# V's bias in the first group: from one-row matmuls on TensorE to the VectorE step that empties PSUM

## The chip, the core and the metric

The kernel runs on one core of a Trainium2 chip. Five engines work on their own instruction queues, each in the order in which the program lists them: TensorE (PE in the profile; its weight loads are PEld), VectorE (DVE), ScalarE (ACT), GpSimd (POOL) and SyncE (SP), which only starts transfers between the chip's memory and SBUF here. The metric is device time in microseconds (us) of one execution; less is better.

## The reference

One graph attention layer over 128 samples of 128 nodes with 768 features, 12 heads of 64, all in float32:

```python
h = jnp.maximum(_layernorm(x, axis=-1), 0.0)
q, k, v = split_heads(h @ Wq + bq), split_heads(h @ Wk + bk), split_heads(h @ Wv + bv)
scores = einsum('bhqd,bhkd->bhqk', q, k) / sqrt(HD) + beta * adj
scores = where(adj > 0, scores, -9e15)
x = x + einsum('bhqk,bhkd->bhqd', softmax(scores), v)
```

The change concerns `h @ Wv + bv` for the first 4 samples, and a preparation of the three weight matrices that is done once.

## The kernel before

**Groups and slices.** The samples are taken in 32 groups of 4 (512 rows). Each group goes through three slices: `qk0` (the first half of the heads' Q and K), `v` (all of V) and `qk1` (the other half of Q and K). Scores, exponentials and the weighted sums of the heads are slipped between the products of later slices.

**Two ways of multiplying.** From the second group on, each slice is a Strassen-like scheme: 15 products (`PRODUCTS`, `product_z`, L543) of sums of activation blocks with sums of weight blocks. The first group is multiplied plainly (`plain_slice`, L832), because the sums of the weights do not exist yet. While TensorE does that, the other engines make them (`prepare`, L271), for `qk0`, `v` and `qk1` in turn: 27 steps a slice, of which 12 are sums on VectorE (`sums`, L297, through L305 and L307) and 15 are finishes (`finish`, L309, and `rest`, L283). Each finish fills the remaining seventh parts of one product's weight tile: two small VectorE sums (L284 and L285, 128x128 each) and two GpSimd sums (L289, L290). The products named B01, B21 and B22 use raw weight blocks; for them `rest` first copies three 128x128 blocks (L287 takes two, L288 one), on GpSimd. Of each slice's 15 tiles, 11 in all three together stay in SBUF (`RESIDENT`); the others are written to memory on SyncE's queue (L293) and read back in each later group. In `v` the tiles are finished in the order T9, T12, T11, TX, T2, B01, B21, B22, T6, T1, T0, T7, T4, T13, T10, where the numbers `n` in `PRODUCTS` are 0, 1, 14, 4, 2, 6, 9, 13, 5, 12, 10, 7, 8, 11, 3.

**The order.** From the first group's `v` slice on, the order of each engine's instructions is that of the program, which is written out by hand in slots. A plain slice has 18 slots: 6 result blocks (two rows of samples by three column blocks) of 3 partial products each. After each third of a block, `behind_product` and the `todo` lists put the other engines' work of that slot into their queues. In the `v` slice: slot 0 to 3 one preparation step, after that two a slot; in slots 5 to 12 one of eight loads each of the raw weights of `qk1` (`raw_qk1_piece`, L246 to L249, in turn from Wq and Wk, 288 KB each); rows of a later group are loaded in slots 0, 1, 2 and 6 and summed on ScalarE (`row_stats`, L421 to L423) in slots 5, 7, 9 and 12; the layer norm's moments of the second group in slots 9 and 12 (`moments_1`, `moments_2`, L375 to L398). All these loads and the writes of prepared tiles share SyncE's queue, in that order. The `qk0` slice, ahead of it, is not ordered by hand.

**One block of V.** TensorE sums 24 matmul passes into a pair of PSUM banks (L855; there are four such pairs in rotation, `take` and `give`). After the first third, two matmuls with one row of ones as weights and the bias as data add the bias to the two halves (L860; float32 takes each in two passes, so four instructions are listed). At the end ScalarE copies the block to SBUF (L871) and the pair is free again. Blocks of Q and K get their bias in the ScalarE step that copies them out (L877). In later groups V's bias is added by VectorE out of PSUM (L573).

**What follows.** The `qk1` slice of the first group multiplies by the raw weights that the eight loads brought: within each third of a block, first all of Wq's part, then all of Wk's. Its preparation starts in slot 16 of the `v` slice with a sum over both. Then the second group begins with L559, whose activation sums VectorE makes at L476.

Of the kernel before, what the change touches and what calls it, by code (L numbers as in the profile page):

```python
# [10 lines left out]
F32 = mybir.dt.float32  # L11
# [3 lines left out]
ALU = mybir.AluOpType  # L15
AX = mybir.AxisListType

P = 128
HEADS = 12
GRP = 4  # L20
# [108 lines left out]
def direct(ctx, tc, x, adj, wq, bq, wk, bk, wv, bv, beta, out, bad):  # L129
# [10 lines left out]
    nc = tc.nc  # L140
    B, N, D = x.shape
    HD = D // HEADS
# [12 lines left out]
    const = ctx.enter_context(tc.tile_pool(name="const", bufs=1))  # L155
# [40 lines left out]
    for g in range(2):  # L196
        t = xg[0, g]
# [6 lines left out]
    mean8 = flat(spot + P, spot + 2 * P).rearrange("p (a i) -> p a i", i=SQ)  # L204
    nhalf = const.tile([P, 1], F32, name="nhalf")
    nc.gpsimd.memset(nhalf, -0.5)
    ones = const.tile([P, P], F32, name="ones")
    nc.gpsimd.memset(ones, 1.0)
    tiny = const.tile([P, 1], F32, name="tiny")
    nc.gpsimd.memset(tiny, TINY)  # L210
# [3 lines left out]
    NS = 2 * NG + 1  # L214
    seen = const.tile([P, NS], F32, name="seen")

    over = const.tile([P, NS + 24], F32, name="over")
# [50 lines left out]
    def quarters(t):  # L268
        return t[:, 0:6].rearrange("p (c z) n -> p c z n", c=2)[:, :, 0:2]

    def prepare(sl):  # L271

        def home(name):
            n = [i for i, p in enumerate(PRODUCTS) if p[1] == name][0]
            if (sl, n) in resident:
                return resident[sl, n]
            made_in[0] += sl != "qk1"
            if sl != "qk1" and made_in[0] % 8 in (2, 5, 7):
                t = work.tile([P, 2, W], F32, tag="e", name=f"prep_{sl}_{n}", bufs=3)
                return t.rearrange("p i w -> p (i w)")[:, 0:7 * P].rearrange("p (z n) -> p z n", n=P)  # L280
            return work.tile([P, 7, P], F32, tag="T", name=f"prep_{sl}_{n}", bufs=RING)

        def rest(n, t, b11, b12, b22, b=None):  # L283
            nc.vector.tensor_tensor(t[:, 6], b12, b11, ALU.subtract)  # L284
            nc.vector.tensor_tensor(t[:, 2], b22, b12, ALU.add)  # L285
            if b is not None:
                nc.gpsimd.tensor_copy(t[:, 0:2], b[:, 0])  # L287
                nc.gpsimd.tensor_copy(t[:, 3], b[:, 1, 0])  # L288
            nc.gpsimd.tensor_tensor(t[:, 4], t[:, 1], t[:, 6], ALU.add)  # L289
            nc.gpsimd.tensor_tensor(t[:, 5], t[:, 0], t[:, 4], ALU.subtract)  # L290
            if (sl, n) not in resident:
                k = kept[sl, n] = dram.tile([P, 7, P], F32, name=f"kept_{sl}_{n}")
                nc.sync.dma_start(k, t)  # L293

        made = {}

        def sums(name):  # L297
            for out, a, b, sign in SUMS_B:
                if out == name:
                    if out not in made:  # L300
                        made[out] = home(out)
                    at = [quarters(made[q]) if q in made else wt[sl, q] for q in (a.strip("-"), b)]
                    op = ALU.add if sign > 0 else ALU.subtract
                    if a[0] == "-":
                        nc.vector.scalar_tensor_tensor(quarters(made[out]), at[0], -1.0, at[1], op0=ALU.mult, op1=op)  # L305
                    else:
                        nc.vector.tensor_tensor(quarters(made[out]), at[0], at[1], op)  # L307

        def finish(name):  # L309
            n = [i for i, p in enumerate(PRODUCTS) if p[1] == name][0]  # L310
            if name in made:
                t = made[name]
                rest(n, t, t[:, 3], t[:, 4], t[:, 1])
            else:
                t, b = home(name), wt[sl, name]
                rest(n, t, b[:, 1, 0], b[:, 1, 1], b[:, 0, 1], b)

        steps = []
        for first, then_finish in PREPARED:
            for name in first:  # L320
                steps.append(lambda name=name: sums(name))
            if sl == "qk1" and first[0] == "T0":
                steps += [load_T, load_T]
            for name in then_finish:
                steps.append(lambda name=name: finish(name))
        return steps
# [28 lines left out]
    bv_b = const.tile([P, D], F32, name="bv_b")  # L355
# [164 lines left out]
    def turn():  # L520

        while between and next(between[0], None) is None:
            between.popleft()
# [4 lines left out]
    def home_qk(G, sl, r, j, zones=False):  # L528
        t = home_of[G, sl, r, j] = homes.popleft()
        return t if zones else t[:, 0:4].rearrange("p (i g) n -> p i (g n)", i=2)  # L530
# [275 lines left out]
    def trail():  # L806
        while trailing:
            trailing.popleft()()

    def behind_product(at, todo):  # L810
        pending = [masking.popleft() for _ in range(len(masking))]
        for f in pending:
            f()
        for f in todo.get(at, ()):
            f()
        while weighing:
            weighing.popleft()()
        overdue()
# [13 lines left out]
    def plain_slice(G, sl, todo, rows=(0, 1)):  # L832

        n = 0
        row0 = None
        for r in rows:
            for j in range(3):
                row0 = last if (r, j) == (1, 0) and sl == "qk0" else row0
                bank = take()
                p = bank[:, :, 0:H2]  # L840

                parts = (slice(0, N), slice(N, H2)) if sl == "qk0" and r == j == 0 else (slice(0, H2),)
                for at, k in [(at, k) for at in parts for k in range(3)]:
                    a, b = A[G, f"A{r}{k}"], wt[sl, f"B{k}{j}"]
                    for i in range(2):
                        for c in range(2):
                            lhs, rhs = b[:, c, i], a[:, c, at]
                            if sl == "v":
                                lhs, rhs = a[:, c, i * N:(i + 1) * N], b[:, c].rearrange("p i n -> p (i n)")
                            for q in range(0, P, HD) if sl == "qk1" else (slice(0, P),):  # L850
                                q = slice(q, q + HD) if sl == "qk1" else q
                                with ExitStack() as behind:
                                    if sl == "qk0" and r == 1:
                                        behind.enter_context(tc.issue_after(row0.ins))
                                    last = nc.tensor.matmul(p[q, i, at], lhs[:, q], rhs, start=(k == 0 and c == 0),  # L855
                                                            stop=(c == 1), skip_group_check=True)
                            turn()
                    if sl == "v" and k == 0:
                        for i in range(2):
                            nc.tensor.matmul(p[:, i], ones[0:1], bv_b[0:1, j * 2 * P:(j + 1) * 2 * P], start=False,  # L860
                                             stop=True, skip_group_check=True)
                    if at is not parts[-1]:
                        if k == 1:
                            with tc.issue_after(last.ins):
                                second()
                        continue
                    if k == 2:
                        if sl == "v":
                            t = vt[G, sl, r, j] = vring[nv[0] % len(vring)]
                            nv[0] += 1  # L870
                            nc.scalar.copy(t.rearrange("p (g h) e -> p g h e", g=2)[:, :, :, 0:HD],  # L871
                                           p.rearrange("p g (h d) -> p g h d", d=HD))
                        else:
                            t = qk[G, sl, r, j] = home_qk(G, sl, r, j)
                            oc = j + 3 * int(sl[2])
                            for i in range(2):
                                nc.scalar.activation(t[:, i, :], p[:, i, :], AF.Identity, bias=bqk[:, i, oc:oc + 1])  # L877
                        give(bank)
                    behind_product(n, todo)
                    trail()  # L880
                    for f in todo.get((n, "post"), ()):
                        f()
                    n += 1
# [163 lines left out]
    for n in range(5, 18):  # L1047
        then(n, after, step, 2)
    plain_slice(0, "qk0", todo)

    ordered = ctx.enter_context(ExitStack())
# [16 lines left out]
    for g, at in enumerate((5, 7, 9, 12)):  # L1068
        then((at, "post"), row_stats, 2, g)
    then((14, "post"), add_raw, 1)  # L1070
    plain_slice(0, "v", todo)

    todo.clear()
# [92 lines left out]
        part()  # L1166

    pf = take()
    nc.tensor.matmul(pf[0:1, 0, 0:NS + 24], ones[:, 0:1], over, start=True, stop=True)
    nc.vector.tensor_reduce(bad, pf[0:1, 0, 0:NS + 24], AX.X, ALU.max)  # L1170
    ordered.close()

# [128 lines left out]
```

## Time and profile before

| | |
|---|---|
| time, median of 3 runs | 2682.6 us (2680.27 to 2682.84) |
| the profiled execution's own time | 2680.71 us |
| its span | 2678.9 us |
| TensorE busy | 2652.9 us (99%) |
| VectorE, ScalarE, GpSimd busy | 2179.0, 1749.4, 2072.5 us |
| mean granted TensorE clock | 0.998 |
| first group: `qk0`, `v`, `qk1` on TensorE | about 10 to 46, 46 to 86, 86 to 123 us |

Times in the profile's rows are counted from the span's start. A row of the timeline gives start, duration, engine, line, operation, output and inputs, and how many instructions were merged; in brackets stands how long the engine stood idle before it and for whom it waited. "PEldq" and "SPq" are the sequencers of TensorE's weight loads and of SyncE. `sbig` is the tile that holds the raw weights, among others; `pair` is a pair of PSUM banks; `kept_v` is the memory copy of a prepared tile.

### The profile page before, as it was taken

To read this page: it belongs to the slowest core of one execution; us is meant where nothing else is said; L and a number is where in the kernel's file an instruction comes from. 1 tells how busy PE (TensorE), PEld (TensorE's weight loads), DVE (VectorE), ACT (ScalarE), POOL (GpSimd) and SP (SyncE) were. 2 spreads that over 40 slices of the span, in tenths; PEclk is the share of its full clock that TensorE was granted. 3 is DMA by queue.
4 is the path that set the end of the run, shared out by engine and by line. 5 is a ranking of instruction groups with operands and counts; after the bars stand their busy time and mean duration, and the time that the engine had idled before them with its cause. 6 is when DMAs were issued, how large, how long until landed. Compare 5 with 4: busy or idle time off the path is not lost.

```text
span 2678.9 us, 121522 instructions
## 1 busy us (share of the span) xinstructions
PE 2652.9 (99%) x52051; PEld 2564.7 (96%) x52051; DVE 2179.0 (81%) x2701; ACT 1749.4 (65%) x4608; POOL 2072.5 (77%) x3043
## 2 busy tenths in 40 slices
PE   9999999999999999999999999999999999999998
PEld 8799999999999999999999999999999999999997
DVE  6877888878888788888788887788887888877885
ACT  2567766676666677666766666776667676667654
POOL 5877778877778777788777787777887777877774
PEclk9999999999999999999999999999999999999999
DMA  9888888989888998889898888988898988888875
GB/s 238 283 261 282 275 270 277 277 265 284 276 271 273 267 279 273 273 277 279 265 281 279 270 272 271 283 274 270 277 277 266 283 277 271 272 274 276 257 240 163
DMA packets 530341, 721.71 MB, mean 269 GB/s; under 512 B 105980, under 2 KB 374024, under 8 KB 529800
## 3 DMA queue, kind: packets, MB, share of 16 engines
q1 hardware_dynamic: 528640, 713.12, 86.7%
q8 instruction: 411, 6.73, 1.0%
q10 hardware_dynamic: 1160, 0.79, 0.2%
q14 instruction: 130, 1.06, 0.1%
HBM read 647.73 MB, written 66.05 MB: 266 GB/s over the span
## 4 chain that ended last, share of the span: by engine, by line
PE 45%; POOL 29%; ACT 13%; issue 5%; DMA 4%; DVE 3%; SPq 0%; POOLq 0%; ACTq 0%; DVEq 0%
PE pair L559 34%; PE pair L695 4%; POOL v L616 4%; PE pair L638 3%; POOL v L615 3%; PE pair L855 3%; POOL A L481 3%; POOL home L614 3%; ACT x L450 3%; ACT e L648 3%; POOL home L601 2%; POOL home L603 2%; ACT home L577 2%; ACT home L579 2%; POOL v L612 2%
## 5 line engine op out<-in xcount | busy, mean ns | idle before, releaser
L583 DVE TENSOR_TENSOR home<-home,pair 128x896 f32<-128x896 f32 x810 | 860.7, 1076 | 273.4 <-PE pair L559 220.7
L559 PE MATMUL pair<-sbig,T_qk 128*64 128x128 f32 x13020 | 833.0, 273 | 1.8 <-DVE sbig L476 0.9
L559 PEld LDWEIGHTS pair<-sbig,T_qk 128*64 128x64 f32 x13020 | 708.2, 137 | 11.6 <-issue 6.4
L559 PE MATMUL pair<-A,T_qk 128*64 128x128 f32 x6944 | 465.6, 273 | 0.4 <-ACT e L707 0.4
L601 POOL TENSOR_TENSOR home<-home 128x256 f32<-128x256 f32 x298 | 246.5, 827 | 268.6 <-DVE home L583 260.1
L678 ACT ACTIVATE e<-e,sm 128x64 f32<-128x64 f32 x1512 | 382.2, 346 | 109.5 <-DVE sm L666 109.5
L559 PE MATMUL pair<-T_v,sbig 128*64 128x128 f32 x6944 | 415.1, 274 | 0.6 <-DMA T_v<-kept_v 0.3
L695 PE MATMUL pair<-v,e 128*64 128x65 f32 x6048 | 401.7, 221 | 6.3 <-DVE e L646 5.9
L577 ACT ACTIVATE home<-pair 128x640 f32<-128x640 f32 x325 | 231.4, 712 | 262.5 <-PE pair L559 201.6
L559 PEld LDWEIGHTS pair<-T_v,sbig 128*64 128x64 f32 x6944 | 380.7, 137 | 12.9 <-issue 10.6
L559 PEld LDWEIGHTS pair<-A,T_qk 128*64 128x64 f32 x6944 | 377.2, 137 | 5.4 <-ACT e L707 4.8
L695 PEld LDWEIGHTS pair<-v,e 128*64 128x64 f32 x6048 | 355.9, 137 | 16.4 <-DVE e L646 12.7
L559 PE MATMUL pair<-sbig,res_qk 128*64 128x128 f32 x4340 | 288.3, 273 | 0.0
L604 POOL TENSOR_TENSOR home<-home 128x256 f32<-128x256 f32 x298 | 238.2, 799 | 23.4
L602 POOL TENSOR_TENSOR home<-home 128x256 f32<-128x256 f32 x298 | 229.8, 771 | 23.4
L559 PEld LDWEIGHTS pair<-sbig,res_qk 128*64 128x64 f32 x4340 | 234.5, 137 | 5.3 <-issue 5.2
L705 ACT ACTIVATE sm<-pair,tiny 128x8 f32<-128x8 f32 x189 | 49.4, 261 | 284.6 <-PE pair L695 284.5
L450 ACT ACTIVATE x<-x,block 128x192 f32<-128x192 f32 x480 | 232.0, 554 | 0.0
L603 POOL TENSOR_TENSOR home<-home 128x128 f32<-128x128 f32 x298 | 213.4, 716 | 23.4
L646 DVE SCALAR_TENSOR_TENSOR e<-pair,biasT 128x1024 f32<-128x1024 f32 x189 | 225.0, 1216 | 2.9 <-PE pair L638 2.8
L648 ACT ACTIVATE e<-e 128x1024 f32<-128x1024 f32 x189 | 193.8, 1066 | 50.2 <-DVE e L646 46.9
L481 POOL TENSOR_TENSOR A<-A 128x256 f32<-128x256 f32 x186 | 168.6, 906 | 56.5 <-DVE A L471 56.5
(201 smaller groups left out, 4598.8 us busy)
## 6 DMA issues: line engine op xcount, KB each, us to landing
T_qk<-kept_qk SPq DMA_DIRECT2D x713, 448.0 KB, 4.8
T_v<-kept_v SPq DMA_DIRECT2D x341, 448.0 KB, 5.6
xo<-in_x_dram SPq DMA_DIRECT2D x189, 256.0 KB, 4.9
out_dram<-xo SPq DMA_DIRECT2D x189, 256.0 KB, 6.0
x<-in_x_dram SPq DMA_DIRECT2D x248, 192.0 KB, 6.2
sbig<-in_x_dram SPq DMA_DIRECT2D x116, 384.0 KB, 3.4
kept_qk<-prep_qk SPq DMA_DIRECT2D x23, 448.0 KB, 3.1
adj<-in_adj_dram SPq DMA_DIRECT2D x128, 64.0 KB, 3.4
```

The source lines that it names most:

```text
L450: nc.scalar.activation(t, t, AF.Relu, bias=shift[G, n], scale=rstd[G, n])
L481: e.tensor_tensor(t[:, 0:2], t[:, 7:8].to_broadcast([P, 2, P]), t[:, 5:7], ALU.subtract)
L559: nc.tensor.matmul(p[q:q + HD, at, :], lhs[:, q:q + HD], rhs, start=(first and at % 4 == 0), stop=True, skip_group_check=True)
L577: nc.scalar.activation(t[:, 0:5], p[:, 0:5], AF.Copy, scale=float(sign))
L583: nc.vector.tensor_tensor(t, t, p[:, 0:7], op)
L601: e.tensor_tensor(t[:, 1:4:2], t[:, 1:4:2], twice(5), ALU.add)
L602: e.tensor_tensor(t[:, 2:5:2], t[:, 2:5:2], twice(1), ALU.add)
L603: e.tensor_tensor(t[:, 4], t[:, 4], t[:, 6], ALU.add)
L604: e.tensor_tensor(t[:, 0:7:6], t[:, 0:7:6], twice(2), ALU.add)
L648: trailing.append(lambda: nc.scalar.activation(e, e, AF.Exp, scale=1.0 / ISCALE))
L678: nc.scalar.activation(o[:, r, b, 0:HD], pa[:, r, b, 0:HD], AF.Copy, scale=t[:, 1, r, b:b + 1])
L695: nc.tensor.matmul(pa[q:q + HD, 2 * g + i, :], k[:, q:q + HD], vt[G, "v", r, h // 4][:, 4 * g + h % 4, :], start=True, stop=True, skip_gro ...
```

## The change

Four edits, all in the first group's part:

- The one-row bias matmuls of the `v` slice are removed; the block is emptied by one VectorE addition of the bias out of PSUM where ScalarE copied it.
- In `rest`, the raw weight copies go from GpSimd to ScalarE, in all three slices.
- In `rest`, for the `v` slice's products with odd `n` (T12, B21, B22, T6, T7, T13 and T10), the second small sum goes from VectorE to GpSimd.
- The tile of ones shrinks from 128 columns to 1; its other use, a sum over partitions at the very end, needs one.

```diff
-    ones = const.tile([P, P], F32, name="ones")
+    ones = const.tile([P, 1], F32, name="ones")
     nc.gpsimd.memset(ones, 1.0)
...
             nc.vector.tensor_tensor(t[:, 6], b12, b11, ALU.subtract)
-            nc.vector.tensor_tensor(t[:, 2], b22, b12, ALU.add)
+            (nc.gpsimd if sl == "v" and n % 2 else nc.vector).tensor_tensor(t[:, 2], b22, b12, ALU.add)
             if b is not None:
-                nc.gpsimd.tensor_copy(t[:, 0:2], b[:, 0])
-                nc.gpsimd.tensor_copy(t[:, 3], b[:, 1, 0])
+                nc.scalar.copy(t[:, 0:2], b[:, 0])
+                nc.scalar.copy(t[:, 3], b[:, 1, 0])
             nc.gpsimd.tensor_tensor(t[:, 4], t[:, 1], t[:, 6], ALU.add)
             nc.gpsimd.tensor_tensor(t[:, 5], t[:, 0], t[:, 4], ALU.subtract)
...
-                    if sl == "v" and k == 0:
-                        for i in range(2):
-                            nc.tensor.matmul(p[:, i], ones[0:1], bv_b[0:1, j * 2 * P:(j + 1) * 2 * P], start=False,
-                                             stop=True, skip_group_check=True)
...
                             nv[0] += 1
-                            nc.scalar.copy(t.rearrange("p (g h) e -> p g h e", g=2)[:, :, :, 0:HD],
-                                           p.rearrange("p g (h d) -> p g h d", d=HD))
+                            bias = bv_b[:, j * 2 * P:(j + 1) * 2 * P].rearrange("p (h d) -> p h d", d=HD)
+                            nc.vector.tensor_tensor(t.rearrange("p (g h) e -> p g h e", g=2)[:, :, :, 0:HD],
+                                                    p.rearrange("p g (h d) -> p g h d", d=HD),
+                                                    bias[:, None].to_broadcast([P, 2, GRP, HD]), ALU.add)
...
-    nc.tensor.matmul(pf[0:1, 0, 0:NS + 24], ones[:, 0:1], over, start=True, stop=True)
+    nc.tensor.matmul(pf[0:1, 0, 0:NS + 24], ones, over, start=True, stop=True)
```

## The prediction, on record before the result

> **What bounds the kernel now.** I read the page first, then TensorE's waits, then the stretch in which the change lies engine by engine. The page's first part, and TensorE's waits in the first 135 us and in a later stretch:
>
> ```profile
> span 2678.9 us, 121522 instructions
> PE 2652.9 (99%) x52051; PEld 2564.7 (96%) x52051; DVE 2179.0 (81%) x2701; ACT 1749.4 (65%) x4608; POOL 2072.5 (77%) x3043
> ```
> ```profile
> PE pair L957 <- DMA bqk_rows<-in_L_gnn_bk_dram: 1.6, 1, 1.6
> PE pair L939 <- POOL sbig masks.py:199: 1.5, 1, 1.5
> PE pair L389 <- DVE dev L382: 1.0, 1, 1.0
> PE pair L559 <- DVE sbig L476: 0.9, 1, 0.9
> ```
> ```profile
> PE pair L695 <- DVE e L646: 0.2, 1, 0.2
> ```
>
> The second fence is all that TensorE waits for in the first 135 us, the third all from 135 to 300 us. So once the second group runs, TensorE hardly waits, and what TensorE gains or loses in the first group is carried to the end one for one. The question is only when TensorE gets through 46 to 133 us.
>
> **What the removed matmuls take.** From the chain that ended last, and TensorE's timeline where the `v` slice ends:
>
> ```profile
> 48.39 1.06 PE pair L860 x4
> ...
> 81.04 1.06 PE pair L860 x4
> ```
> ```profile
> 82.02 3.72 PE L855 MATMUL pair<-sbig,A 128*128 128x256 f32 x16
> 85.67 3.67 PE L855 MATMUL pair<-A,sbig 128*64 128x256 f32 x32
> ```
>
> Six blocks, each 1.06 us: 6.36 us of TensorE's time, between other matmuls without a gap. This is the most that the removal can bring, 0.24% of the run. I call a change within 0.2% (5.4 us) no change; it is about what a measurement of this kernel can tell.
>
> **What TensorE meets earlier.** At 85.67 it starts `qk1`, with raw weights that eight loads bring during the `v` slice. In each third of a block Wq's part comes first (8 of the 32 matmuls of the row above, 8 x 3.67/32 = 0.92 us), so Wk is needed at 86.59. TensorE's sequencer, VectorE's first use of the same weights, SyncE's last issues and the time to landing:
>
> ```profile
> L855 PEldq EVENT_SEMAPHORE  x18: 51/51/1742, 8.5 to 84.3; - x18
> ```
> ```profile
> 86.20 0.69 DVE L307 TENSOR_TENSOR prep_qk<-sbig 128x512 f32<-128x512 f32 x1 [4.32 <-DMA sbig<-in_L_gnn_Wk_dram]
> ```
> ```profile
> 76.62 0.56 SPq L249 DMA_DIRECT2D sbig<-in_L_gnn_Wq_dram  x1
> 77.28 0.43 SPq L293 DMA_DIRECT2D kept_v<-prep_v  x1
> 77.76 0.43 SPq L249 DMA_DIRECT2D sbig<-in_L_gnn_Wk_dram  x1
> ```
> ```profile
> DMA to landing us min/median/max: 5.9/6.4/8.2
> ```
>
> The last Wk load is issued at 77.76 and lands 8.2 us later; VectorE idles 4.32 us for it, until 86.20. One of TensorE's 18 sequencer waits lasts 1.742 us, and the last of them begins at 84.3: together 86.0, the same moment. Today that wait is covered by matmuls already queued. TensorE thus uses Wk at 86.59, 0.39 us after it is there. Without the bias matmuls it would want Wk at 80.23 and would stand until 86.20. Of 6.36 us, 5.97 go into this new wait: -0.39.
>
> **Does the last load land at another time?** It is issued behind the write of T6 (77.28), which waits for GpSimd's last sum of T6. GpSimd and VectorE there, and the whole stretch by windows:
>
> ```profile
> 74.29 0.79 POOL L290 TENSOR_TENSOR prep_v<-prep_v 128x128 f32<-128x128 f32 x1
> 75.84 0.45 POOL L289 TENSOR_TENSOR prep_v<-prep_v 128x128 f32<-128x128 f32 x1 [0.76 <-DVE prep_v L285]
> ```
> ```profile
> 69.10 0.19 DVE L378 TENSOR_REDUCE mean<-pair 128x16 f32<-128x32 f32 x1 [0.88 <-ACT v L871]
> ```
> ```profile
> 46.50:85.70 39.20, 39.20 (x179) 31.07 (x177) 33.39 (x80) 15.84 (x37) 33.95 (x55) 1.00 0.92 303
> 79.30:86.00 6.70, 6.70 (x33) 5.05 (x33) 2.57 (x10) 3.91 (x9) 6.31 (x11) 1.00 0.96 269
> ```
>
> T6 waits for VectorE (0.76 us), so VectorE's load counts. The prices, from the nearest rows:
>
> ```profile
> L573 DVE TENSOR_TENSOR home<-bv_b,pair x160: 412/421/423, 155.4 to 2616.1; 128x256 f32<-128x256 f32 x160
> L583 DVE TENSOR_TENSOR home<-home,pair x810: 1026/1086/1091, 129.0 to 2665.7; 128x896 f32<-128x896 f32 x162
> L285 DVE TENSOR_TENSOR prep_v<-sbig x3: 277/541/542, 65.7 to 67.3; 128x128 f32<-128x128 f32 x3
> L289 POOL TENSOR_TENSOR prep_v<-prep_v x11: 452/461/1005, 62.6 to 85.8; 128x128 f32<-128x128 f32 x11
> L287 POOL COPY prep_v<-sbig x3: 393/399/859, 67.9 to 71.8; 128x256 f32<-128x256 f32 x3
> L288 POOL COPY prep_v<-sbig x3: 292/298/755, 68.2 to 72.6; 128x128 f32<-128x128 f32 x3
> ```
>
> - The new VectorE step is 128x512 out of PSUM: between 421 ns for 256 columns and 1086 for 896, so 421 + 256 x 665/640 = 0.69 us. Four of the six (slots 2, 5, 8, 11) stand ahead of T6's finish on VectorE: +2.8.
> - The second sums of T12, B21 and B22 leave VectorE before that: 0.28 to 0.54 each by L285's row, -1.1. The 0.88 us for which VectorE waited ahead of L378 goes too: L378 needs a matmul of slot 9, which comes four blocks' bias matmuls earlier. VectorE reaches T6 some 0.8 us later.
> - GpSimd starts T9 one new VectorE step later (+0.7), loses three copy pairs (1.65 + 1.35, -3.0) and gains three sums at 0.46 (+1.4): it is done with B22 0.9 us sooner, and then waits for VectorE at T6.
>
> The last load is issued about 0.8 us later. The transfer engines are at 0.92 to 0.96 of their time, so the landing may hang on the bytes ahead of it alone, and these do not change: 0 to +0.8; I take +0.4. The copies on ScalarE (12 beside this slice's 6) are hidden: it is busy 15.84 of 39.20 us and loses six copies of 0.58; without that cover they would cost some 0.5 us each.
>
> [...]
>
> **The emptying itself.** Today's copies already come late, behind other ScalarE work, without a wait of TensorE:
>
> ```profile
> 83.86 0.56 ACT L871 COPY v<-pair 128x512 f32<-128x512 f32 x1
> ```
>
> The sixth block's bias matmuls start at 81.04, one third of a block (8 x 0.23 = 1.9 us) after the fifth is complete, so this fifth block waited from 79.2 to 83.86. VectorE will be some us late in the same way, and with four pairs in rotation I cost that at nothing: a missing pair, or a wait at L389 for VectorE like the 1.0 us above, would lie inside the wait for Wk, whose end depends on neither. If that cover is gone (Wk early), about 1 us of it shows.
>
> **What six idle microseconds do to TensorE.** Fills at the start and after, and windows near the end (columns: length, then busy time of PE, PEld, DVE, ACT, POOL, then granted clock, share of the transfer engines, GB/s):
>
> ```profile
> 1.50 6.52 PE L939 MATMUL pair<-sbig 128*128 128x128 f32 x30 [1.50 <-POOL sbig masks.py:199]
> ...
> 8.96 1.73 PE L939 MATMUL pair<-sbig 128*128 128x128 f32 x14
> ```
> ```profile
> 2666.00:2668.00 2.00, 0.29 (x8) 0.04 (x4) 1.90 (x4) 0.00 (x0) 0.00 (x0) 1.00 0.52 143
> 2668.00:2670.00 2.00, 1.65 (x36) 1.10 (x38) 1.89 (x6) 0.78 (x2) 0.00 (x0) 1.00 0.19 58
> 2670.00:2672.00 2.00, 1.76 (x32) 1.57 (x31) 1.08 (x7) 0.89 (x3) 0.00 (x0) 0.50 0.03 8
> ```
>
> The first 30 fills take 217 ns each, later ones 124: TensorE starts slow and stays so for 6.52 us, which costs 6.52 - 30 x 0.124 = 2.8 us. Near the end a stretch with 1.7 us of idle is followed by a granted clock of 0.50. The new wait, from 79.3 with 0.9 us of Wq's part in it, idles three times as long. I take that the clock falls and that TensorE pays as at the start, +2.8; the ends are 0 (it holds) and 3.3 (half of 6.52).
>
> [...]
>
> **The second group's first sums.** TensorE's one wait there, and VectorE's idle time before it:
>
> ```profile
> 133.08 1.75 PE L559 MATMUL pair<-sbig,T_qk 128*64 128x128 f32 x28 [0.92 <-DVE sbig L476]
> ```
> ```profile
> 118.27 1.60 DVE L476 TENSOR_TENSOR sbig<-A,A 128x896 f32<-128x896 f32 x1 [2.10 <-POOL A L483]
> ```
> ```profile
> 97.22 0.46 POOL L287 COPY prep_qk<-sbig 128x256 f32<-128x256 f32 x1
> ...
> 103.85 0.76 POOL L288 COPY prep_qk<-sbig 128x128 f32<-128x128 f32 x1
> ```
>
> VectorE's chain from 86.20 on shifts with the landing (+0.4) and holds the last emptying (+0.7), but its 2.10 us wait for GpSimd shrinks: GpSimd loses three copy pairs here too, about 3 us. So VectorE is about 1 us early and TensorE 2.8 us late, and the 0.92 goes: -0.9. If GpSimd gains nothing, the wait shrinks by TensorE's lateness all the same.
>
> **Sum**, against the profiled execution (2680.71 us, span 2678.9): -6.36 + 5.97 + 0.4 + 2.8 - 0.9 = +1.9, so 2682.6. That execution lies 1.9 us below the median of the runs; carried to the median, 2682.6 + 1.9 = 2684.5 us: no change that can be told. With all ends: -0.39 - 0.9 = -1.3 to -0.39 + 0.8 + 3.3 = +3.7, so 2681.3 to 2686.3.
>
> **Rivals.**
> - The clock holds through the wait. For it: the early wait of 1.6 us for L957 lies in this window, of whose 3.40 us TensorE is busy 2.24, and the clock stays at 1.00. Without +2.8: 2681.7.
>
> ```profile
> 13.60:17.00 3.40, 2.24 (x19) 2.25 (x20) 0.00 (x0) 0.23 (x2) 0.64 (x3) 1.00 1.02 230
> ```
>
> - The load comes as much earlier as TensorE does. For it: SyncE waits for GpSimd between these loads, and GpSimd loses work. Against it: the busy transfer engines, and that T6 hangs on VectorE, which gains work. It needs a landing before 81: then -6.36, 2676.2, faster.
> - Slower: a GpSimd sum is starved while VectorE works without a break. It has happened:
>
> ```profile
> 36.05 4.27 POOL L289 TENSOR_TENSOR prep_qk<-prep_qk 128x128 f32<-128x128 f32 x1 [5.92 <-DVE prep_qk L285]
> ```
>
>   against a median of 0.46. VectorE will be busier in the `v` slice. One such stall on T6 or before it holds the last Wk load back by 3.8 us: 2684.5 + 3.8 = 2688.3. It decides from 3.5 us on. Against it: no such row between 46 and 86.
>
> **Chances.** Forecast 0.52, clock holds 0.18, early load 0.12, starved sum 0.18. So faster by over 0.2%: 0.12; within: 0.70; slower: 0.18. The range 2678.5 to 2689.5 takes in all but the early load and a longer stall.
>
> **What would show it.** Right: no L860; six VectorE steps near 0.69 us at the new line; TensorE idle between 79 and 86 until "DMA sbig<-in_L_gnn_Wk_dram"; a granted clock of 0.50 after it; VectorE's first `qk1` sum still at 86 to 87; no wait for L476. Wrong: `qk1` starting near 80 on TensorE, a landing away from 86 by more than 1 us, or TensorE waiting for a pair.

## The result, and the profile after

The changed kernel takes 2707.32 us (median of 6 runs, 2705.32 to 2714.43) against 2682.72 us (2680.27 to 2685.09) for the kernel before: ratio 1.0091, 95% interval 1.008 to 1.0102. It is slower by 24.6 us, outside the predicted range. Its profiled execution took 2705.32 us, with a span of 2703.5 us. Times below are medians of all executions of a kernel, while the recorded ratios leave out the few that took 3389 us and more and compare with the kernel before as measured beside it (2682.7 to 2684.2 us); they differ by up to 0.0016 from the quotient of two medians.

The first group went much as forecast. TensorE's timeline of the changed kernel (start, duration, instructions; in brackets the idle time before and who ended it):

```profile
45.53 17.43 PE L855 MATMUL pair<-sbig,A 128*128 128x256 f32 x80
...
70.03 0.31 PE L389 MATMUL pair<-dev,sbig 128*64 128x32 f32 x4 [1.45 <-DVE dev L382]
70.27 8.90 PE L855 MATMUL pair<-sbig,A 128*128 128x256 f32 x40
83.61 1.36 PE L855 MATMUL pair<-A,sbig 128*64 128x256 f32 x8 [4.44 <-DMA sbig<-in_L_gnn_Wq_dram]
85.41 3.91 PE L855 MATMUL pair<-A,sbig 128*64 128x256 f32 x24 [0.44 <-issue]
...
123.14 6.28 PE L559 MATMUL pair<-sbig,T_qk 128*64 128x128 f32 x112
...
132.80 1.75 PE L559 MATMUL pair<-sbig,T_qk 128*64 128x128 f32 x28 [0.67 <-DVE sbig L476]
```

and the rows of the kernel before at which `v` and the second group begin:

```profile
46.50 1.89 PE L855 MATMUL pair<-sbig,A 128*128 128x256 f32 x8
...
123.16 6.28 PE L559 MATMUL pair<-sbig,T_qk 128*64 128x128 f32 x112
```

L860 is gone. `v` begins 0.97 us earlier and takes 83.61 - 4.44 - 45.53 = 33.64 us where it took 85.67 - 46.50 = 39.17; with its wait at L389 taken out that is 6.98 us less. TensorE gives this back: 1.45 us at L389, 4.44 and 0.44 us at the start of `qk1`, and 1.60 us because the first 32 matmuls of `qk1` take 1.36 + 3.91 = 5.27 us where they took 3.67. In all -0.97 - 6.98 + 1.45 + 4.44 + 0.44 + 1.60 = -0.02: the second group begins at 123.14 where it began at 123.16. Up to there the change is worth nothing, and the 24.6 us are lost behind it, in stretches whose instructions no edit touches.

Three more rows of the changed kernel from this place: SyncE's last load of the raw weights, VectorE's first sum for `qk1`, and the window behind TensorE's wait (length, then busy time of PE, PEld, DVE, ACT, POOL, then granted clock, share of the transfer engines, GB/s):

```profile
78.02 0.43 SPq L249 DMA_DIRECT2D sbig<-in_L_gnn_Wk_dram  x1
```
```profile
85.54 0.93 DVE L307 TENSOR_TENSOR prep_qk<-sbig 128x512 f32<-128x512 f32 x1 [3.17 <-POOL prep_v L289]
```
```profile
84.30:87.70 3.40, 2.96 (x16) 1.51 (x14) 2.07 (x3) 3.40 (x9) 3.11 (x6) 0.50 0.55 215
```

This Wk load lands 7.3 us after its issue, at 85.3. The 0.44 us that the profile lists under "issue" lie between the 8 matmuls with Wq and those with Wk, and end at 85.41: they fit a wait for this load, though the profile does not name it. VectorE's first sum, which needs the load too, begins at 85.54; the profile puts the end of its idle time down to GpSimd. Behind the wait the granted clock is 0.50 for 3.4 us. An estimate from these two numbers: at half the clock for 3.4 us TensorE loses some 1.7 us, which agrees with the 1.60.

The kernel before and the changed one by windows (columns as above):

```profile
0.00:135.00 135.00, 129.90 (x1101) 105.29 (x1105) 105.54 (x231) 52.98 (x133) 90.47 (x154) 1.00 0.90 259
135.00:2500.00 2365.00, 2356.32 (x47600) 2299.71 (x47596) 1943.74 (x2286) 1603.47 (x4224) 1867.96 (x2721) 1.00 0.89 274
```
```profile
0.00:135.00 135.00, 123.87 (x1089) 101.71 (x1093) 108.72 (x230) 54.34 (x145) 87.85 (x143) 0.99 0.91 258
135.00:2500.00 2365.00, 2339.26 (x47102) 2277.53 (x47094) 1920.07 (x2261) 1590.45 (x4179) 1844.87 (x2693) 1.00 0.90 272
```

From 135 to 2500 us TensorE stands still for 2365 - 2356.32 = 8.7 us before and 25.7 us after, and it issues 498 matmuls fewer in the same time, some 1% of 47,600. The idle time is not all of the loss: TensorE's busy time per matmul goes from 2356.32 us / 47,600 = 49.50 ns to 49.66, at a granted clock of 1.00 in both, which for 47,102 matmuls is another 7.6 us. With the 17.0 us more of idle time this makes the 24.6; what stretches the busy time no run shows. TensorE's longest sums of waits from 135 to 2300 us, before and after (sum in us, times, longest):

```profile
PE pair L695 <- DVE e L646: 5.4, 24, 0.2
PE pair L638 <- issue: 0.7, 1, 0.7
PE pair L559 <- issue: 0.6, 2, 0.3
```
```profile
PE pair L559 <- issue: 10.3, 11, 1.8
PE pair L559 <- DMA T_qk<-kept_qk: 6.1, 13, 0.9
PE pair L638 <- issue: 1.6, 3, 0.6
```

TensorE now waits for the prepared weights that are read back from memory, 6.1 us in 13 waits, which it hardly did before (less than the 0.6 us of the third row). The transfers' rows say the same (KB of one, median us from issue to landing), before and after:

```profile
T_qk<-kept_qk SPq DMA_DIRECT2D x713, 448.0 KB, 4.8
xo<-in_x_dram SPq DMA_DIRECT2D x189, 256.0 KB, 4.9
x<-in_x_dram SPq DMA_DIRECT2D x248, 192.0 KB, 6.2
adj<-in_adj_dram SPq DMA_DIRECT2D x128, 64.0 KB, 3.4
```
```profile
T_qk<-kept_qk SPq DMA_DIRECT2D x713, 448.0 KB, 5.0
xo<-in_x_dram SPq DMA_DIRECT2D x189, 256.0 KB, 5.3
x<-in_x_dram SPq DMA_DIRECT2D x248, 192.0 KB, 7.1
adj<-in_adj_dram SPq DMA_DIRECT2D x128, 64.0 KB, 3.7
```

The same transfers, as many and as large, land later in the whole run, the loads of `x` most. The change was described as four edits in the first group's part, but one of them reaches beyond it: the tile of ones. It was 512 bytes in each partition and is now 4, for which 32 are reserved in the compiled kernel; so the tiles placed behind it in SBUF lie 480 bytes lower. In the compiled kernels the tiles `x`, `xo`, `adj`, `e`, `A` and `T` start at multiples of 256 bytes before, and 32 bytes past one after.

A transfer is carried out in pieces. From the trace's records of single pieces between 300 and 2500 us I took the mean time of each size (a load of `x` goes in pieces of 768 bytes, one of `adj` in pieces of 128; the counts are those of the kernel before):

```
piece      pieces    before    after     (mean ns of one)
128 B       58752      13.0     13.8
512 B      165358      27.5     27.4
768 B       55296      55.1     64.8
3072 B      13696     138.3    141.4
3584 B     117200     174.4    173.6
```

The pieces of 768 bytes take 9.7 ns longer: 55,296 x 9.7 ns / 16 engines = 33.5 us for each transfer engine. The busy time of all pieces, over 16 engines, went from 2357 to 2392 us.

### The profile page after: what moved, and what is told of

Same layout as the page of the kernel before. It is cut to its first block, busy times and chain, and to the rows that moved or that the text cites. A ratio compares the mean times of both kernels' runs of the same rounds, so it can differ in the third digit from the quotient of the medians.

```text
span 2703.5 us, 121486 instructions
## 1 busy us (share of the span) xinstructions
PE 2654.1 (98%) x52027; PEld 2563.0 (95%) x52027; DVE 2181.7 (81%) x2700; ACT 1751.3 (65%) x4620; POOL 2069.2 (77%) x3032
## 4 chain that ended last, share of the span: by engine, by line
PE 65%; POOL 14%; DMA 9%; ACT 5%; issue 3%; DVE 2%; SPq 1%; ACTq 0%; POOLq 0%; DVEq 0%
PE pair L559 53%; PE pair L638 5%; PE pair L695 5%; DMA T_qk<-kept_qk 4%; DMA x<-in_x_dram 3%; POOL v L616 2%; POOL v L615 1%; POOL home L614 1%; POOL A L481 1%; PE pair L855 1%; ACT x L450 1%; ACT e L648 1%; ACT home L577 1%; POOL home L601 1%; ACT home L579 1%
## 5 line engine op out<-in xcount | busy, mean ns | idle before, releaser
L559 PE MATMUL pair<-T_v,sbig 128*64 128x128 f32 x6944 | 420.6, 274 | 11.7 <-issue 10.2
L604 POOL TENSOR_TENSOR home<-home 128x256 f32<-128x256 f32 x298 | 240.1, 806 | 23.4
L602 POOL TENSOR_TENSOR home<-home 128x256 f32<-128x256 f32 x298 | 230.7, 774 | 23.4
L603 POOL TENSOR_TENSOR home<-home 128x128 f32<-128x128 f32 x298 | 212.4, 713 | 23.4
```

Of the source, the lines that this page charges most:

```text
L559: nc.tensor.matmul(p[q:q + HD, at, :], lhs[:, q:q + HD], rhs, start=(first and at % 4 == 0), stop=True, skip_group_check=True)
L602: e.tensor_tensor(t[:, 2:5:2], t[:, 2:5:2], twice(1), ALU.add)
L603: e.tensor_tensor(t[:, 4], t[:, 4], t[:, 6], ALU.add)
L604: e.tensor_tensor(t[:, 0:7:6], t[:, 0:7:6], twice(2), ALU.add)
```

## The experiments

The first runs ask which edit carries the loss: the addresses, which only the smaller tile of ones moves, or the moved work of the three others.

**The tile of ones kept wide.**

```diff
-    ones = const.tile([P, 1], F32, name="ones")
+    ones = const.tile([P, P], F32, name="ones")
...
-    nc.tensor.matmul(pf[0:1, 0, 0:NS + 24], ones, over, start=True, stop=True)
+    nc.tensor.matmul(pf[0:1, 0, 0:NS + 24], ones[:, 0:1], over, start=True, stop=True)
```

> The changed kernel with the tile of ones 128 columns wide again, so that every tile behind it has its old address; the other three edits stay. If the 25 us come from the addresses (all tiles behind `ones` lie 480 bytes lower after the change, 32 past a multiple of 64 where they were on one), this run is back at 2681 to 2684 us: the first group alone gives about no change (TensorE enters the second group at 123.14 with the change and at 123.16 without). If they come from the moved work of the first group, it stays at 2705 to 2710.

2683.92 us, ratio 0.9998 (0.9987 to 1.0009): the whole loss is gone with three of the four edits in. Its timeline also shows the first group undisturbed by the addresses:

```profile
69.46 0.31 PE L389 MATMUL pair<-dev,sbig 128*64 128x32 f32 x4 [0.38 <-DVE dev L382]
69.70 8.90 PE L855 MATMUL pair<-sbig,A 128*128 128x256 f32 x40
83.56 6.77 PE L855 MATMUL pair<-A,sbig 128*64 128x256 f32 x32 [4.96 <-DMA sbig<-in_L_gnn_Wq_dram]
...
133.81 1.75 PE L559 MATMUL pair<-sbig,T_qk 128*64 128x128 f32 x28 [0.67 <-DVE sbig L476]
```

The 32 matmuls behind the wait take 6.77 us, 3.1 more than before. The windows there (columns as above) show why: after 5 us without work the granted clock is 0.50 for 6 us, nearly twice as long as in the changed kernel.

```profile
79.00:83.50 4.50, 0.00 (x0) 0.00 (x0) 2.80 (x8) 1.48 (x4) 4.26 (x6) 0.92 1.03 250
83.50:86.00 2.50, 2.42 (x10) 1.18 (x12) 0.32 (x1) 2.50 (x7) 2.27 (x6) 0.50 0.47 182
86.00:89.50 3.50, 3.50 (x20) 2.19 (x18) 3.38 (x6) 3.15 (x8) 3.26 (x5) 0.50 0.98 260
89.50:93.00 3.50, 3.50 (x56) 2.38 (x54) 3.50 (x11) 0.00 (x0) 2.32 (x6) 0.99 0.79 310
```

**The shift alone, in the kernel before.**

```diff
     ones = const.tile([P, P], F32, name="ones")
     nc.gpsimd.memset(ones, 1.0)
+    pad = const.tile([P, 8], F32, name="pad")
+    nc.gpsimd.memset(pad, 0.0)
```

> The kernel before, with nothing but an unused tile of 32 bytes a partition behind `ones`: every tile from there on starts 32 past a multiple of 64. Addresses: 2703 to 2710 us, and the 768-byte transfers into x as slow as in the changed kernel. Moved work: no change, 2682.7.

2706.58 us, ratio 1.0071 (1.0045 to 1.0097; four runs). An unused tile of 32 bytes makes the kernel before about as slow as the changed one. With the run above this decides it: the address is enough, and without it there is no loss. The window of this kernel that answers to those above, and its busy times in all:

```profile
135.00:2500.00 2365.00, 2337.78 (x47036) 2275.41 (x47034) 1915.82 (x2259) 1587.27 (x4175) 1839.32 (x2687) 1.00 0.90 271
```
```profile
PE 2661.7 (98%) x52051; PEld 2567.3 (95%) x52051; DVE 2177.5 (80%) x2701; ACT 1748.4 (65%) x4608; POOL 2068.5 (76%) x3044
```

VectorE, ScalarE and GpSimd are no longer busy than before (2179.0, 1749.4 and 2072.5 us), so it is not these engines that the shifted addresses slow. TensorE is busy 8.8 us longer (2652.9 before) with the same 52,051 matmuls.

**How the loss depends on the address.** The changed kernel with an unused tile behind the narrow `ones`, here of 32 bytes:

```diff
     ones = const.tile([P, 1], F32, name="ones")
     nc.gpsimd.memset(ones, 1.0)
+    pad = const.tile([P, 8], F32, name="pad")
+    nc.gpsimd.memset(pad, 0.0)
```

> The changed kernel with the narrow tile of ones and 32 bytes more behind it: all tiles lie 448 bytes lower than before, a multiple of 64 but not of 128, 256 or 512. If what counts is the multiple of 64: 2681 to 2684. If it is a coarser one: 2700 or more. Moved work: 2705 to 2710.

and with `[P, 24]` and `[P, 56]` in place of `[P, 8]` (96 and 224 bytes):

> The changed kernel with 96 bytes more behind the narrow tile of ones: all later tiles 384 bytes lower than before, x on a multiple of 128 that is none of 256. The first four runs gave 768-byte transfers into x of 55 ns (old address, a multiple of 256), 62 (odd multiple of 64) and 65 (32 past one). If a multiple of 128 is enough: 2681 to 2685. If it takes 256: some 2695 as with 64. A smooth dependence on the multiple: about 2688 to 2692.

> The changed kernel with 224 bytes more behind the narrow tile of ones: all later tiles 256 bytes lower than before, x on a multiple of 512. If only the remainder counts: 2681 to 2685. If the very addresses of before were lucky for another reason (a distance to the tiles ahead of `ones`, which do not move): 2690 or more.

All in one table, with the bytes by which the tiles start past a multiple of 256, the mean time of a 768-byte piece, and TensorE's idle time from 135 to 2500 us in the profiled execution:

```
kernel            x   others   time (us)   ratio to before (95%)        768 B (ns)   PE idle (us)
before            0      0      2682.7      1                             55.1           8.7
after            32     32      2707.3      1.0091 (1.008 to 1.0102)      64.8          25.7
before_shift32   32     32      2706.6      1.0071 (1.0045 to 1.0097)     65.2          27.2
after_pad64      64     64      2698.3      1.0054 (1.0039 to 1.0069)     62.5          19.2
after_pad128    128    128      2689.2      1.0014 (0.9996 to 1.0033)     59.3          13.0
after_pad256      0      0      2684.8      1.0001 (0.9983 to 1.0019)     54.3          10.0
```

Pieces and idle time rise together: 128 bytes past the multiple of 256 costs some 6 us of run by the medians, though its interval still reaches to none; 64 bytes past some 15, 32 bytes past some 24. So neither a multiple of 64 nor one of 128 restores the time, as two of the expected cases had it; the loss shrinks step by step. The last row's `x` lies on a multiple of 512 where that of the kernel before lies 256 past one; that brings nothing more. The rows from which the idle time of the first and last pad is taken:

```profile
135.00:2500.00 2365.00, 2345.84 (x47258) 2285.30 (x47256) 1926.69 (x2270) 1596.09 (x4202) 1851.10 (x2701) 1.00 0.89 272
```
```profile
135.00:2500.00 2365.00, 2355.01 (x47558) 2298.01 (x47554) 1940.20 (x2285) 1600.65 (x4220) 1864.60 (x2719) 1.00 0.89 274
```

**Which tiles.** Two unused tiles around `x`, first in the changed kernel with 32 bytes each:

```diff
         else:
+            if (G, r) == (0, 1):
+                nc.gpsimd.memset(work.tile([P, 8], F32, tag="pad0", name="pad0", bufs=1), 0.0)
             t = work.tile([P, 2 * NB, QD], F32, tag="x", name=f"x_{G}_{r}", bufs=1)
+            if (G, r) == (0, 1):
+                nc.gpsimd.memset(work.tile([P, 8], F32, tag="pad1", name="pad1", bufs=1), 0.0)
```

> The changed kernel, with only the x tile put back on a multiple of 64 (32 bytes in front of it, 32 behind); all other tiles stay where the change put them. x's loads are the only large group of transfers whose landing got clearly later (6.2 to 7.1 us). If they carry the loss: 2681 to 2686. If the read-back weight tiles, xo or the rest carry it: 2698 or more.

2694.77 us, 1.0044 (1.0032 to 1.0057). The compiled kernel has `x` 64 and the others 96 bytes past a multiple of 256, pieces of 768 bytes at 61.1 ns. About half of the loss stays, between the two cases expected, so it does not hang on whether `x` alone is a multiple of 64. Cleaner are the two next ones: `x` back on its multiple of 256 with the others 32 off (480 bytes ahead of `x`, 32 behind: `[P, 120]` and `[P, 8]`), and the kernel before with `x` alone 32 off (`[P, 8]` and `[P, 56]`).

> The changed kernel with x alone put back at exactly its old address; the tiles behind it stay 32 past a multiple of 64. If x's loads carry all of the loss: 2681 to 2685. If about half is carried by other tiles (the small adjacency loads, xo, the weight tiles): 2690 to 2697, little better than the run with x on an odd multiple of 64 (2694.8).

2689.82 us, 1.0016 (0.9998 to 1.0034); pieces of 768 bytes at 55.7 ns again, pieces of 128 bytes at 13.8.

> The reverse on the kernel before: x alone 32 past a multiple of 64, the tiles behind it on multiples of 256. If x's loads carry the loss: 2700 to 2707. If the others do: 2683 to 2688. With the run above this shows whether the two parts add up to 24 us.

2695.03 us, 1.0039 (1.002 to 1.0058); 768-byte pieces at 63.1 ns, 128-byte pieces at 13.0. So `x` carries the larger part. Shifted alone it costs 12.2 of the 24 us (against its own 2682.9; some 10 by the ratio), where either 17 or more or nearly nothing was expected; put back alone it leaves 7 of 24, or some 4 by the ratio, whose interval reaches to none. What the other tiles carry by themselves is therefore not clear of noise. By the medians the two parts make 19; that the rest comes from both together was not tried.

**The first group's wall.** With the addresses out of the way, TensorE's 6.4 us are lost to the wait for the raw loads of `qk1` and to the clock behind it. Can that be kept, and do the other two edits of the first group matter? The raw loads earlier, with the wide tile and in the kernel before:

```diff
     for n in range(8):
-        then(5 + n, raw_qk1_piece, n)
+        then(5 + n // 4, raw_qk1_piece, n)
```

> The wide tile of ones kept, all three edits of the first group in, and the eight raw loads of the third slice issued in slots 5 and 6 of the second slice instead of slots 5 to 12, ahead of the writes of the kept V tiles. Theory of the load wall: in the run with the wide tile the 6.4 us that TensorE saved were lost again as 5.0 us of waiting for these loads (83.56) and 3.1 us of slower clock behind it. With the loads landed before 79 us neither arises: the wait on the load goes, the 32 matmuls of L855 behind it take 3.7 us as before, and what then stops TensorE is VectorE's chain, whose first qk1 sum moves from 85.7 to about 82, so some 4 of the 8 us are kept: 2678 to 2680 us, ratio 0.998 to 0.999. Rival, the time of the first group is set by VectorE's and GpSimd's work alone: TensorE waits as long at L476 near 133 instead, 2682 to 2684 us. Rival, the writes of the kept tiles come late by the 3 us that the loads now take on SyncE's queue, and the third slice waits on them: 2685 to 2687 us.

2687.01 us, 1.0012 (1.0003 to 1.0021): not faster, and the third of the expected cases. TensorE's rows:

```profile
80.97 3.67 PE L855 MATMUL pair<-A,sbig 128*64 128x256 f32 x32 [2.58 <-DMA sbig<-in_L_gnn_Wq_dram]
...
105.60 6.66 PE L855 MATMUL pair<-A,sbig 128*64 128x256 f32 x36 [5.31 <-ACT home L875]
```

The first wait is halved, the matmuls behind it keep their pace (32 in 3.67 us again, 115 ns each), and then a new wait of 5.31 us stands at 105.6, with slower matmuls behind it (36 take 6.66 us, 185 ns each). ScalarE, which empties the pair that TensorE waits for, had just waited for VectorE, and VectorE for a write:

```profile
83.60 0.69 DVE L307 TENSOR_TENSOR prep_v<-sbig,prep_v 128x512 f32<-128x512 f32 x1 [4.75 <-DMA kept_v<-prep_v]
```
```profile
104.01 0.72 ACT L500 ACTIVATE adj<-adj,beta_s 128x512 f32<-128x512 f32 x1 [3.25 <-DVE biasT L499]
```

VectorE's step waits until the write that frees its tile has landed. The writes of L293 (seven of them are issued from 74.30 on) land much later after their issue with the raw loads ahead of them; from 60 to 95 us, in the run with the wide tile alone and in this one:

```profile
DMA to landing us min/median/max: 2.8/4.1/7.0
```
```profile
DMA to landing us min/median/max: 3.1/9.2/10.8
```

In the kernel before, the transfer engines' share was already 0.92 from 46.5 to 85.7 us and 0.96 from 79.3 to 86: here one transfer came earlier by putting others behind it. That VectorE's 4.75 us are what reaches TensorE at 105.6 is read from these rows and was not tested by a run.

> The kernel before with the same earlier issue of the eight raw loads and nothing else. Load wall: TensorE reached these loads 1 us or more after they had landed before the change, so nothing is gained, 2682 to 2683.5 us, ratio 1.000. Were the earlier loads good by themselves, it would gain what the run with the wide tile and early loads gains (2678 to 2680); were they harmful to the writes behind them, 2685 or more.

2685.18 us, 1.0005 (0.9996 to 1.0014): no change that can be told, so the earlier loads are not good by themselves, though TensorE has a wait of 3.4 us at the same place in `qk1` (for ScalarE's L877) which it did not have.

The bias edit alone (the wide tile; copies on GpSimd, all small sums on VectorE, as before):

```diff
-            (nc.gpsimd if sl == "v" and n % 2 else nc.vector).tensor_tensor(t[:, 2], b22, b12, ALU.add)
+            nc.vector.tensor_tensor(t[:, 2], b22, b12, ALU.add)
...
-                nc.scalar.copy(t[:, 0:2], b[:, 0])
-                nc.scalar.copy(t[:, 3], b[:, 1, 0])
+                nc.gpsimd.tensor_copy(t[:, 0:2], b[:, 0])
+                nc.gpsimd.tensor_copy(t[:, 3], b[:, 1, 0])
```

> The bias edit alone: the wide tile of ones, copies back on GpSimd, the seven sums back on VectorE. Load wall: the loads land when they did, TensorE waits for them as with all three edits, 2682.5 to 2684.5 us, ratio 1.000. Rival, the other two edits make room that the six longer VectorE evictions need: without them VectorE is 2.0 us (7 x 0.28) later at the first sums of the third slice and the wait at L476 near 133 grows by about that: 2685 to 2687 us.

2688.84 us, 1.0015 (1.0006 to 1.0024): the rival's side, and beyond it. TensorE's waits from 60 to 135 us:

```profile
PE pair L855 <- DVE prep_v L285: 2.8, 1, 2.8
PE pair L389 <- DVE dev L382: 2.3, 1, 2.3
PE pair L855 <- issue: 0.8, 1, 0.8
```

and its one row of the second group's first sums:

```profile
135.45 1.75 PE L559 MATMUL pair<-sbig,T_qk 128*64 128x128 f32 x28 [1.58 <-DVE sbig L476]
```

VectorE is now late at L389 (2.3 us) and at L476 (1.58). At that row the kernel is 135.45 - 133.81 = 1.6 us behind the one with all three edits. This agrees with the expectation that the moved copies and sums make room on VectorE, which the six steps that empty PSUM take; which of the two edits does it was not tried. With the bias edit alone the whole run is some 0.15% slower than before, with all three it is level (0.9998, though the two intervals overlap).

Last, the loads of rows for group 2 put behind the raw loads:

```diff
-        then(5 + n, raw_qk1_piece, n)
+        then(5 + n // 2, raw_qk1_piece, n)
...
-    for g, at in enumerate((0, 1, 2, 6)):
+    for g, at in enumerate((7, 8, 9, 13)):
         then((at, "post"), load_row, 2, g)
-    for g, at in enumerate((5, 7, 9, 12)):
+    for g, at in enumerate((12, 14, 16, 17)):
         then((at, "post"), row_stats, 2, g)
```

> All three edits of the first group and the wide tile of ones; the four loads of x rows for group 2 (384 KB each, three of them ahead of the raw weights) go from slots 0, 1, 2, 6 of the second slice to slots 7, 8, 9, 13 with their sums from 5, 7, 9, 12 to 12, 14, 16, 17, and the raw loads go two to a slot from slot 5. Theory of the full transfer engines: between 55 and 85 us they are busy nearly all the time, so a load comes earlier only by what is put behind it. The three row loads are 1.15 MB, 3 to 4 us at the 297 to 347 GB/s of this stretch: the last raw load lands about 80 instead of 83.5 us, TensorE waits 1 to 2 us instead of 5.0, its clock stays at 1.00 (the 32 matmuls of L855 take 3.7 us), and the kept V tiles are written as early as before: 2678.5 to 2681 us if nothing else is late. Rival, ScalarE's sums of the rows now run into its eight norms of L450 at 82 us and delay the evictions of the third slice, as the late writes did in the run with early loads: 2684 to 2687 us. Rival, TensorE's wait returns in full at L476 near 133, set by VectorE: 2682 to 2684 us.

2687.22 us, 1.0009 (1.0 to 1.0018): no gain. No trace shows where the time goes in an execution of this kernel that takes 2687 us. The time speaks against the gain; it lies above both rivals, far nearer to that of the delayed evictions (2684 to 2687), but without a trace at this time the cause stays open. No kernel tried is faster than the one before.

## Why the prediction was wrong

**The step that failed** is one that the prediction did not take: the fourth edit, the smaller tile of ones, has no term in the sum at all. Its price was put at nothing without a reason, and so the sum ends with the second group ("what TensorE gains or loses in the first group is carried to the end one for one"). That holds for work; it does not hold for a shift of nearly every tile that transfers write. The measured term is +24 us (23.4 by putting the tile back, 2707.32 against 2683.92; by the shift alone 1.0071, some 19, or 23 by the medians). None of the rivals had its mechanism: the one that gives a slower time, a starved sum on GpSimd, would have been a loss in the first group.

The steps that were taken, against the runs with the wide tile and of the changed kernel:

- **Removal, -6.36.** The instructions are gone and `v` takes 6.98 us less, waits left out. Right, and 0.6 us too small.
- **The new wait, +5.97 for Wk.** 4.96 us with the wide tile, 4.44 + 0.44 in the changed kernel. It ends at 83.6, for Wq's loads; VectorE's first `qk1` sum, which needs Wk, stands at 85.68 and 85.54 where 86 to 87 was forecast. So a load holds TensorE, as forecast, but first the other one: the prediction took Wq as already there, though its last load was issued only 1.1 us before Wk's (76.62 and 77.76 in its rows). The wait was put 2.6 us too late, and Wq's part is not done while waiting, but behind the wait.
- **Landing, +0.4.** The last Wk load is issued at 78.02 (77.45 with the wide tile) against 77.76, not 0.8 us later, and the first sum starts 0.7 us (0.5) earlier rather than 0.4 later. The new VectorE step takes 0.68 us (0.69 forecast). The moved sums are dearer on GpSimd than the 0.46 us taken from L289 (below), yet do not hold the loads back: no starved sum appears (the longest of L289's for `v` takes 0.92 us in the changed kernel).
- **The clock, +2.8.** It falls to 0.50 behind the wait and costs 3.1 us with the wide tile, where it stays there for 6 us, and 1.6 us in the changed kernel, where it stays for 3.4. The rival that it holds fell.
- **The wait at L476, -0.9.** It stays: 0.67 us in both. VectorE's chain did not gain on TensorE by what was forecast. A wait at L389 for VectorE came to 0.38 us with the wide tile and 1.45 us in the changed kernel, and cost nothing: TensorE's wait for the load ends at 83.56 and 83.61 all the same, so the one lies inside the other, as the prediction had it.

Together, for the three edits that were costed, the prediction had 2684.5 us; the kernel with exactly these takes 2683.92 (0.7 us above the kernel before beside it, where 1.9 was forecast). The agreement is partly luck, of errors that cancel: a shorter wait, a wait that stays, a dearer clock.

What stays open: how the address slows a piece, and why mainly pieces of 768 bytes show it (of the others only a few: the 99th percentile goes from 13 to 36 ns for pieces of 128 bytes and from 27 to 35 for those of 512). Most of TensorE's added idle time stands under "issue", where the profile names nobody, and 7.6 us do not show as idle time at all; how the slower transfers come to cost TensorE this time is not shown, only that they and the loss come and go together.

## What to carry to other kernels

When an edit changes the size of a tile, look at what lies behind it in SBUF: if the transfer engines are as full as here (0.89 to 0.90), try to keep tiles that transfers fill with rows as short as these 768 bytes at multiples of 256 bytes (there a piece took 54 to 56 ns, off them 59 to 65), and test a change of size by putting an unused tile in its place. And before a matmul is taken off TensorE, find what it meets next: here a load, behind full transfer engines, and a slower clock took back all of the 6.4 us, and moving the load only moved the wait.

## What the runs showed of the hardware beyond that

- Rows of 768 bytes landing in SBUF 32 bytes past a multiple of 256 take 65 ns a piece rather than 54 to 55; 64 past, 62.5; 128 past, 59.3. The means of 3584 and 512 bytes hardly move between the kernel before and the changed one: 174.4 and 173.6, 27.5 and 27.4 ns.
- The small sums moved to GpSimd take either 0.45 or 0.90 us there, the longer as often as not, where I had priced 0.46. The changed kernel's groups of that line (ns, min/median/max):

```profile
L285 POOL TENSOR_TENSOR prep_v<-prep_v x5: 454/901/903, 62.7 to 88.1; 128x128 f32<-128x128 f32 x5
L285 POOL TENSOR_TENSOR prep_v<-sbig x2: 456/679/902, 69.5 to 71.2; 128x128 f32<-128x128 f32 x2
```

- With the transfer engines at a share of 0.93 to 0.99 (the run with the wide tile, 55 to 85 us, in three windows of 10), loads issued earlier made the writes behind them land later (median 9.2 us after issue rather than 4.1): eight loads brought forward freed 2.4 us at one wait (4.96 to 2.58) and cost 5.3 at the next.
